# Fills, transposes, first copies, FFN sums and projection steps in another order: a Macaron block on one Trainium2 core

## The chip, the cores and the metric

The kernel runs on one core of one Trainium2 chip. Its time is the device time in microseconds (us) of one execution; several executions give a median. TensorE is called PE, VectorE DVE, ScalarE ACT, GpSimd POOL, SyncE SP, as in the profile; "ACTq" and "SPq" are the queues on which an engine issues DMAs.

## The reference

One Macaron block over x of shape (2, 1024, 256), all in float32:

```python
x = x + 0.5 * ffn(layernorm(x), w_gate, w_up, w_down)
x = x + attention(layernorm(x), Wq, bq, Wk, bk, Wv, bv, Wo, bo)
x = x + 0.5 * ffn(layernorm(x), w_gate, w_up, w_down)

def ffn(x, ...):                       # 256 -> 1024 -> 256
    h = silu(x @ w_gate) * (x @ w_up)
    h = keep_the_2_largest_of_each_4_neighbours_by_magnitude(h)
    return h @ w_down

def attention(x, ...):                 # 32 heads of 8, 8 key/value heads, causal
    q, k, v = x @ Wq + bq, x @ Wk + bk, x @ Wv + bv
    q, k = rope(q), rope(k)
    p = softmax(mask(q @ k.T / sqrt(8)))
    return concat_heads(p @ v) @ Wo + bo
```

## The kernel before

**Data.** The 2048 tokens are four blocks `tb` of 512 tokens; `xs[tb]` holds a block as four tiles of 128 tokens x 256 columns. Blocks 0 and 1 are sequence 0 (b = 0), blocks 2 and 3 sequence 1.

**Stages.** The first FFN (about 0 to 181 us) runs from a written plan: `l` is a layernorm step (`layernorm_T`: statistics on DVE, `rstd` on POOL, normalization into `xn`, eight 128x128 transposes on PE into one PSUM tile `lnT`, a copy to `xnT`); `g` a gate/up step (`gu`, PE; then sg, h, a on ACT and DVE); `m` a mask step on DVE; `d` the down projection (`o`); `a` its sum into x; `p` a step of the attention's beginning. The first `p` fills qT0, kT0 and vaug0 (`rows`, `sequence`, lines 381 to 398) on POOL and then projects q, k and v of sequence 0. Attention follows in 16 units (b, g), one for each key/value head with its four query heads, in rounds of about 25.6 us; then the second FFN, from about 640 us, with the same steps. The down projection of block 3 in the first FFN is left over for round 0 (`down_slowly`, called `beside_first`).

**A round** is written out as a list of operations, `order`: `p1` are scores of the current unit for the row maxima (PE into a "big" PSUM buffer, DVE `maxima`, line 599), `p2` the transposed scores of the unit before it (PE, then an exponential on ACT, line 665, then POOL's causal mask, line 671, where a block is diagonal), `av` the weighted sums of values (PE, line 692), `shift` transposes the maxima (`mT`, line 626), copies them on ACT (`mrow`) and sends them by four DMAs into rows of qT, and `prep` makes the next unit's qT and kT: eight PE transposes (`hT`), a copy on ACT (`stage`, line 524), then 18 DMAs on SP (lines 529 to 545). A round has 18 `p1` operations. In round 0 there is no unit before, so only `p1`, `prep`, one `shift` and the left-over down projection run: after every second `p1`, two steps of `beside_first`, each four matmuls as the program counts pairs, a group of eight matmul records in the trace. Its two sums into x (`add`, line 327) are on DVE.

**Projection of sequence 1.** In rounds 1 to 7 a generator, `project(1, ...)`, is advanced by one step (`a_step`) at certain operations: layernorm statistics (4 steps), rstd (1), normalization on POOL (4), two transposing steps (`lnT`), four additions of bo, and then for each of four tiles a projection step (`pr`, PE; `raw`, DVE; `values`, ACT) and six POOL steps of rope; 43 steps a block, two blocks. Its steps are taken at `shift`, `prep`, `av`, and two of the `p2`: 15 a round. `lnT` and `pr` use the one buffer of pool `ps_tr`, which `shift` uses too:

```python
if n > 0 and (op[0] in ("av", "shift", "prep") or op in (("p2", 2), ("p2", 9))):
    a_step()
```

**What sets the order.** PE and DVE follow the plan in the FFNs; PE and POOL follow the written order in the rounds; elsewhere a scheduler places instructions, and each engine then works strictly in its order. The "big" PSUM pool has three buffers, `ps_tr` and `ps_acc` (sums `o` of the first half, `av`) one each. DMAs on SP and ACT share eight completion counters in turn, so each waits for the one eight places before it.

**The end.** The last operations are `d3 a d3 a a`: the sum of half a block (128 x 512) on DVE, then one DMA of 256 KB to the output.

Of the kernel before, what the change touches and what calls it, by code (L numbers as in the profile page):

```python
# [1 line left out]

# [6 lines left out]
FP = mybir.dt.float32  # L9
# [3 lines left out]
ALU = mybir.AluOpType  # L13
# [3 lines left out]
P = 128  # L17
B, T, C = 2, 1024, 256
NT = B * T
TB = 512  # L20
NTB = NT // TB
NTT = TB // P
# [12 lines left out]
def macaron_kernel(  # L35
# [17 lines left out]
    nc = tc.nc  # L53
# [3 lines left out]
    lnp = ctx.enter_context(tc.tile_pool(name="ln", bufs=2))  # L57
# [5 lines left out]
    xs = [const.tile([P, NTT, C], FP, name=f"x{tb}") for tb in range(NTB)]  # L63
# [98 lines left out]
    def layernorm_T(tb, make, after=None, halves=False, copy=None):  # L162

        xt = xs[tb]
        mv = small.tile([P, NTT, 2], FP, name=f"mv{tb}", tag="mv")
        for t in range(NTT):
            with ExitStack() as order:
                if after:  # L170
                    order.enter_context(tc.issue_after(after()))
                st = small.tile([P, 6], FP, name=f"st{tb}_{t}", tag="st")
                nc.vector.bn_stats(st, xt[:, t, :])
                nc.vector.bn_aggr(mv[:, t, :], st)
            if after:
                yield
        ve = small.tile([P, NTT], FP, name=f"ve{tb}", tag="ve")
        nc.vector.tensor_scalar(ve, mv[:, :, 1], EPS, None, ALU.add)  # L178
        rstd = small.tile([P, NTT], FP, name=f"rstd{tb}", tag="rstd")
        nc.gpsimd.tensor_tensor(rstd, ve, neg_half, ALU.pow)  # L180
        yield
        xn = lnp.tile([P, NTT, C], FP, name=f"xn{tb}", tag="xn")
        for t in range(NTT):
            (nc.gpsimd if after else nc.vector).tensor_scalar(
                xn[:, t, :],
                xt[:, t, :],
                mv[:, t, 0:1],
                rstd[:, t : t + 1],
                ALU.subtract,
                ALU.mult,  # L190
            )
            if after:
                yield
        if not after:
            yield
        dst = make()
        if not after:
            both = ps_big.tile([P, 2, TB], FP, name=f"lnT{tb}", tag="big")
            for kc in range(2):
                for t in range(NTT):  # L200
                    nc.tensor.transpose(  # L201
                        both[:, kc, bass.ts(t, P)], xn[:, t, bass.ts(kc, P)], ident
                    )
            if halves:
                nc.scalar.copy(dst[:, 0, :], both[:, 0, :])  # L205
                nc.vector.tensor_copy(dst[:, 1, :], both[:, 1, :])
            else:
                (copy or nc.scalar.copy)(dst, both)
        else:
            for kc in range(2):  # L210
                tr = ps_tr.tile([P, TB], FP, name=f"lnT{tb}_{kc}", tag="tr")
                for t in range(NTT):
                    nc.tensor.transpose(
                        tr[:, bass.ts(t, P)], xn[:, t, bass.ts(kc, P)], ident
                    )
                nc.scalar.copy(dst[:, kc, :], tr)
                yield
        if not after:
            yield


    class FFN:
# [94 lines left out]
        def down_slowly(self, tb):  # L317

            for t2 in range(2):
                yield from self.down_half(tb, t2, ps_acc, "acc")  # L320
                self.add()

        def add(self):

            tb, t2, o = self.adds.pop(0)
            part = xs[tb][:, bass.ts(t2, 2), :]
            nc.vector.scalar_tensor_tensor(part, o, 0.5, part, ALU.mult, ALU.add)
            if self.store:
                nc.sync.dma_start(
                    out=out[bass.ts(tb, TB), :].rearrange("(t p) c -> p t c", p=P)[  # L330
                        :, bass.ts(t2, 2), :
                    ],
                    in_=part,
                )

        def run(self, plan, gens, outs=()):

# [35 lines left out]
    def attention(actx, beside_first, beside_last, outs):  # L373
# [7 lines left out]
        def rows(pool):  # L381
            i = len(qTs)
            qT = pool.tile([P, REP // 2, T], FP, name=f"qT{i}")
            nc.gpsimd.memset(qT, 0.0)
            qTs.append(qT)
            kT = pool.tile([P, T], FP, name=f"kT{i}")
            nc.gpsimd.memset(kT, 1.0)
            kTs.append(kT)

        def sequence(pool, part_pool):  # L390
            b = len(vaugs)


            vaug = pool.tile([P, NQT, NKV * VW + 32 - VW], FP, name=f"vaug{b}")
            nc.gpsimd.memset(vaug, 1.0)
            vaugs.append(vaug)
            if part_pool:
                parts.append(part_pool.tile([P, NQT, H + NKV, 2 * D], FR, name=f"part{b}"))
# [93 lines left out]
        class Unit:  # L492
# [15 lines left out]
            def prepare(self):  # L508


                s = f"{self.b}_{self.g}"
                tr = ps_big.tile([P, 2, TB], FP, name=f"hT{s}", tag="big")
                src = parts[self.b][:, :, bass.ts(self.g, REP + 1), :]
                for t in range(NQT):

                    nc.tensor.matmul(  # L516
                        out=tr[0 : 2 * GW, t // NTT, bass.ts(t % NTT, P)],
                        lhsT=src[:, t, :, :].rearrange("p h n -> p (h n)"),
                        rhs=ident_r,
                        start=True,  # L520
                        stop=True,
                    )
                hT = early.tile([P, T], FP, name=f"stage{s}", tag="stage")
                nc.scalar.copy(hT[0 : 2 * GW, :], tr[0 : 2 * GW, :, :].rearrange("p i n -> p (i n)"))
                W = 2 * D
                for s in range(2):

                    lo = s * STRIP + ROWS
                    nc.sync.dma_start(
                        out=self.qT[lo : lo + 2, :, :].rearrange("p i (c n) -> p (i c) n", n=TB // 2),  # L530
                        in_=zeros[:, None, :].to_broadcast([2, 2 * REP, TB // 2]),
                    )
                    for j in range(2):
                        for i in range(2):
                            lo = s * STRIP + j * W + i * D
                            nc.sync.dma_start(
                                out=self.kT[lo : lo + D, :],
                                in_=hT[REP * W + j * D : REP * W + j * D + D, :],
                            )
                        lo = s * STRIP + j * W  # L540
                        for pair in range(2):
                            h = 2 * pair + s
                            nc.sync.dma_start(
                                out=self.qT[lo : lo + W, pair, :], in_=hT[h * W : h * W + W, :]
                            )

# [239 lines left out]
        def parsed(order):  # L786
            return [(op[0], *map(int, op[1:])) for op in map(str.split, order.split(";"))]

        ops = parsed(order)
        first = max(i for i, op in enumerate(ops) if op[0] == "p1" and op[1] < 3)  # L790
        units = [(b, g) for b in range(B) for g in range(NKV)]
        made = {}
# [46 lines left out]
        def a_step():  # L839
            while beside and next(beside[0], beside) is beside:  # L840
                beside.pop(0)

        def round_(n, prev, cur):
            nxt = Unit(*units[n + 1]) if n + 1 < len(units) else None
            if n == 1:
                beside.append(second)
            if nxt is not None and nxt.b == 1:
                for _ in second:
                    pass
            firsts = 0  # L850
            for i, op in enumerate(ops):
                step(op, prev, cur, nxt)
                if i == first and cur is not None:
                    cur.negated(0)
                if n == 0 and i == first:

                    nc.scalar.activation(warm, cur.maxima[0][:, 0, 6:7], AF.Exp, scale=0.0)
                if n == 0 and op[0] == "p1":
                    firsts += 1
                    for _ in range(2 * (firsts % 2)):  # L860
                        next(beside_first, None)
                if n > 0 and (op[0] in ("av", "shift", "prep") or op in (("p2", 2), ("p2", 9))):
                    a_step()
                if n > NKV and op == ("av", 5) and divisions:
                    next(divisions.pop(0))
            return cur, nxt
# [138 lines left out]
```

## Time and profile before

| | us |
|---|---|
| median of 3 runs (range) | 828.13 (827.17 to 828.27) |
| the profiled execution | 822.23 |
| its span, first to last instruction | 820.5 |
| mean granted TensorE clock in it | 0.996 |
| PE busy / DVE busy / ACT busy / POOL busy | 781.6 / 655.6 / 426.1 / 235.2 |

The profile is one execution, with every instruction's start and duration. A row of the timeline gives start and duration in us, engine, source line, operation, output and inputs, the number of merged instructions, and in brackets the engine's idle time before it with what ended it. The chain of waits follows the work that ended last back to the start, and adds up its time by engine. "PEclk" or "granted clock" is the share of full TensorE clock that the chip allowed.

### The profile page before, as it was taken

How to read it: one execution, taken by the hardware profiler on the slowest of the kernel's cores; microseconds unless marked ns; L12 is line 12 of the kernel's file. 1: busy time of each engine (PE TensorE's matmuls, PEld its weight loads, DVE VectorE, ACT ScalarE, POOL GpSimd, SP SyncE). 2: the span in 40 equal slices, each digit the busy share in tenths (PEclk: the TensorE clock that was granted, in tenths of full speed). 3: DMA queues.
4: the chain of work that ended last, by engine and by line, in shares of the span. 5: the costliest groups of instructions: out<-in, count | busy, mean ns of one | idle time of the engine just before them, and what ended most of it. 6: DMA issues, size and time to landing. Idle time of an engine off the chain costs nothing.

```text
span 820.5 us, 13946 instructions
## 1 busy us (share of the span) xinstructions
PE 781.6 (95%) x5344; PEld 424.6 (52%) x5344; DVE 655.6 (80%) x870; ACT 426.1 (52%) x529; POOL 235.2 (29%) x443
## 2 busy tenths in 40 slices
PE   4999999999899999999999999999999999999998
PEld 2447574477444544444445444454445445657466
DVE  4797989898968887788889888888885479788692
ACT  1331313211667677768787778878777423122210
POOL 3000193911435555464223322233223100000000
PEclk9999999999999999999999999999999999999999
DMA  8100000022203212311333333322202200000001
GB/s 277 31 0 2 0 2 0 0 39 43 37 21 66 39 45 57 67 25 47 68 68 63 93 73 67 56 46 51 56 30 94 71 1 16 1 26 1 15 11 51
DMA packets 30994, 36.03 MB, mean 44 GB/s; under 512 B 12880, under 2 KB 20944, under 8 KB 30928
## 3 DMA queue, kind: packets, MB, share of 16 engines
q1 hardware_dynamic: 29312, 32.26, 17.6%
q10 hardware_dynamic: 1616, 2.88, 1.0%
q8 instruction: 42, 0.69, 0.3%
q14 instruction: 24, 0.20, 0.1%
HBM read 10.75 MB, written 10.75 MB: 26 GB/s over the span
## 4 chain that ended last, share of the span: by engine, by line
PE 75%; DVE 16%; ACT 4%; POOL 1%; issue 1%; SPq 1%; DMA 1%; DVEq 0%; ACTq 0%; POOLq 0%
PE gu L251 22%; PE av L692 16%; PE o L306 10%; PE s L655 9%; PE s L570 9%; DVE maxima L599 7%; ACT e L665 3%; PE pr L461 2%; PE oo L739 2%; PE lnT L201 1%; PE s L585 1%; PE hT L516 1%; DVE h L291 1%; DVE h L261 1%; DVE sg L260 1%
## 5 line engine op out<-in xcount | busy, mean ns | idle before, releaser
L599 DVE TENSOR_REDUCE maxima<-s 128x2 f32<-128x1024 f32 (+2 forms) x288 | 343.8, 1222 | 62.1 <-PE s L570 44.6
L665 ACT ACTIVATE e<-s 128x1024 f32<-128x1024 f32 x288 | 287.6, 1023 | 93.9 <-PE s L655 86.0
L671 POOL TENSOR_SCALAR_AFFINE_SELECT e<-e 128x256 f32<-128x256 f32 (+1 forms) x224 | 98.2, 451 | 216.7 <-ACT e L665 216.0
L692 PE MATMUL av<-e,vaug 128*32 128x512 f32 (+3 forms) x1536 | 156.6, 496 | 0.0
L570 PE MATMUL s<-kT,qT 64*128 64x512 f32 (+3 forms) x768 | 132.8, 382 | 14.1 <-ACT e L665 11.8
L655 PE MATMUL s<-qT,kT 64*128 64x512 f32 (+3 forms) x768 | 134.2, 394 | 4.4 <-DVE maxima L599 3.5
L251 PE MATMUL gu<-xnT,wg_sb 128*128 128x512 f32 x256 | 121.9, 599 | 0.7 <-ACT xnT L205 0.7
L251 PE MATMUL gu<-xnT,wu_sb 128*128 128x512 f32 x256 | 120.3, 592 | 0.0
L306 PE MATMUL o<-wd_sb,h 128*128 128x256 f32 x512 | 114.4, 381 | 0.1
L570 PEld LDWEIGHTS s<-kT,qT 64*128 64x128 f32 x768 | 68.0, 186 | 81.3 <-ACT e L665 36.8
L306 PEld LDWEIGHTS o<-wd_sb,h 128*128 128x128 f32 x512 | 96.3, 190 | 17.0 <-issue 3.8
L655 PEld LDWEIGHTS s<-qT,kT 64*128 64x128 f32 x768 | 67.2, 185 | 63.5 <-DVE maxima L599 34.3
L259 ACT ACTIVATE sg<-gu 128x512 f32<-128x512 f32 x64 | 38.1, 595 | 117.9 <-PE gu L251 117.9
L262 ACT ACTIVATE a<-h 128x512 f32<-128x512 f32 x64 | 40.3, 630 | 99.4 <-DVE h L261 99.4
L260 DVE TENSOR_TENSOR sg<-sg,gu 128x512 f32<-128x512 f32 x64 | 43.7, 684 | 47.7 <-ACT sg L259 47.6
L251 PEld LDWEIGHTS gu<-xnT,wu_sb 128*128 128x128 f32 x256 | 48.7, 190 | 61.5 <-issue 61.5
L251 PEld LDWEIGHTS gu<-xnT,wg_sb 128*128 128x128 f32 x256 | 48.6, 192 | 54.6 <-issue 49.7
L180 POOL TENSOR_TENSOR rstd<-ve,neg_half 128x4 f32<-128x4 f32 x12 | 12.2, 1016 | 189.7 <-DVE ve L178 187.8
L692 PEld LDWEIGHTS av<-e,vaug 128*32 128x32 f32 x1536 | 34.0, 108 | 49.5 <-issue 37.8
L261 DVE TENSOR_TENSOR h<-sg,gu 128x512 f32<-128x512 f32 x64 | 44.0, 687 | 2.2
L291 DVE SCALAR_TENSOR_TENSOR h<-w,h 128x512 f32<-128x512 bf16 x64 | 44.0, 750 | 0.0
L585 PE MATMUL s<-half_id,half_mask 64*128 64x64 bf16 (+1 forms) x768 | 43.7, 203 | 0.0
(76 smaller groups left out, 562.8 us busy)
## 6 DMA issues: line engine op xcount, KB each, us to landing
qT<-stage SPq DMA_DIRECT2D x128, 64.0 KB
avs<-oT SPq DMA_DIRECT2D x32, 256.0 KB
kT<-stage SPq DMA_DIRECT2D x128, 32.0 KB
qT<-mrow SPq DMA_DIRECT2D x128, 4.0 KB
heads<-avs SPq DMA_DIRECT2D x16, 128.0 KB
out<-x SPq DMA_DIRECT2D x8, 256.0 KB
wu_sb<-in_wu SPq DMA_DIRECT2D x2, 512.0 KB
wg_sb<-in_wg ACTq DMA_DIRECT2D x2, 512.0 KB
```

The source lines that it names most:

```text
L251: nc.tensor.matmul(out=gu[:, i, :], lhsT=w_sb[:, kc, gb, j, :], rhs=self.xnT[tb][:, kc, :], start=(kc == 0), stop=(kc == 1),)
L260: nc.vector.tensor_tensor(sg, sg, gu[:, 0, :], ALU.mult)
L261: nc.vector.tensor_tensor(h[:, j, :], sg, gu[:, 1, :], ALU.mult)
L291: nc.vector.scalar_tensor_tensor(h[:, j, :], w[:, j, :], at, h[:, j, :], op, ALU.mult)
L306: nc.tensor.matmul(out=o[:, i, :], lhsT=self.hms[tb][k // 4][:, k % 4, bass.ts(2 * t2 + i, P)], rhs=self.wd_sb[:, k // 4, k % 4, :], start ...
L570: nc.tensor.matmul(out=to[:, i, s, bass.ds(col, n)], lhsT=self.qT[strip, pair, bass.ts(qt, P)].bitcast(FR), rhs=self.kT[strip, bass.ds(kc ...
L585: nc.tensor.matmul(out=last.rearrange("p (t n) -> p t n", n=P)[:, :, bass.ts(h, STRIP)], lhsT=half_mask[strip, h, :], rhs=half_id[strip, N ...
L599: ins = nc.vector.tensor_reduce(dst, src, AX.X, ALU.max, negate=True)
L655: nc.tensor.matmul(out=to[:, i, s, bass.ds(col, n)], lhsT=self.kT[strip, bass.ts(kb, P)].bitcast(FR), rhs=self.qT[strip, pair, bass.ds(q0, ...
L665: nc.scalar.activation(e, to, AF.Exp, scale=SCALE)
L671: nc.gpsimd.affine_select(out=first, in_=first, pattern=[[0, 2], [0, len(pairs)], [1, P]], compare_op=ALU.is_ge, fill=0.0, base=0, channel ...
L692: nc.tensor.matmul(out=self.av[32 * i : 32 * i + 32, TB - n : TB], lhsT=vaugs[self.b][:, kb, bass.ds(self.g * VW, 32)], rhs=es[i][:, bass. ...
```

## The change

1. In `layernorm_T` the eight transposes of a block go tile by tile (t outside, kc inside) instead of one 128-column half after the other.
2. kT0 and vaug0 are filled by DVE instead of POOL.
3. The DMAs that build the first unit's qT and kT go to SP and ACT in turn; those of all other units stay on SP.
4. The two sums of the down projection in round 0 are a scaled copy on ACT and an addition on POOL instead of one DVE instruction. Of its steps, those after the 13th `p1` and later run after the round's last operation.
5. In rounds 1 to 7 no projection step follows `shift` or the two `p2` any more; two follow each of `av` 1, 3, 5 and 7. There are still 15 a round.
6. The last sum of the kernel, and its store, are made for each 128-token tile by itself.

In the built program the fills of kT0 and vaug0 stand on DVE between the fill of `zeros` (right after the sum of `o_0_1`) and the statistics of the attention's first layernorm. On ACT one of the `zeros` DMAs stands in the middle of the first FFN; of the others one stands between the copy `stage_0` and the last Abs, and seven behind that. On PE the last two groups of `o_3_1` stand between the last `p1` of round 0 and the first `p2` of round 1.

```diff
@@ layernorm_T
-            for kc in range(2):
-                for t in range(NTT):
+            for t in range(NTT):
+                for kc in range(2):
                     nc.tensor.transpose(
                         both[:, kc, bass.ts(t, P)], xn[:, t, bass.ts(kc, P)], ident
                     )
@@ FFN.down_slowly
-                self.add()
+                self.add_aside()
+
+        def add_aside(self):
+            tb, t2, o = self.adds.pop(0)
+            part = xs[tb][:, bass.ts(t2, 2), :]
+            half = lnp.tile([P, NTT, C], FP, name=f"half{tb}_{t2}", tag="xn")[:, 0:2, :]
+            nc.scalar.mul(half, o, 0.5)
+            nc.gpsimd.tensor_tensor(part, part, half, ALU.add)
@@ FFN.add
-            part = xs[tb][:, bass.ts(t2, 2), :]
-            nc.vector.scalar_tensor_tensor(part, o, 0.5, part, ALU.mult, ALU.add)
-            if self.store:
-                nc.sync.dma_start(out=..., in_=part)
+            last = self.store and tb == NTB - 1 and t2 == 1
+            for i in range(0, 2, 1 if last else 2):
+                n = 1 if last else 2
+                tiles = bass.ds(2 * t2 + i, n)
+                part = xs[tb][:, tiles, :]
+                nc.vector.scalar_tensor_tensor(
+                    part, o[:, i : i + n, :], 0.5, part, ALU.mult, ALU.add
+                )
+                if self.store:
+                    nc.sync.dma_start(out=..., in_=part)
@@ rows, sequence
-            nc.gpsimd.memset(kT, 1.0)
+            (nc.vector if i == 0 else nc.gpsimd).memset(kT, 1.0)
-            nc.gpsimd.memset(vaug, 1.0)
+            (nc.vector if b == 0 else nc.gpsimd).memset(vaug, 1.0)
@@ Unit.prepare
+                queues = itertools.cycle([nc.sync] if self.b or self.g else [nc.sync, nc.scalar])
-                    nc.sync.dma_start(     # zeros, kT and qT alike
+                    next(queues).dma_start(
@@ round_
+        PAIRS = [("av", k) for k in (1, 3, 5, 7)]
                 if n == 0 and op[0] == "p1":
                     firsts += 1
-                    for _ in range(2 * (firsts % 2)):
-                        next(beside_first, None)
-                if n > 0 and (op[0] in ("av", "shift", "prep") or op in (("p2", 2), ("p2", 9))):
-                    a_step()
+                    if firsts <= 12:
+                        for _ in range(2 * (firsts % 2)):
+                            next(beside_first, None)
+                if n > 0:
+                    for _ in range(2 if op in PAIRS else op[0] in ("av", "prep")):
+                        a_step()
```

## The prediction

> **What bounds the kernel now.** I read the page first, its busy times and its chain of waits.
>
> ```profile
> PE 781.6 (95%) x5344; PEld 424.6 (52%) x5344; DVE 655.6 (80%) x870; ACT 426.1 (52%) x529; POOL 235.2 (29%) x443
> ...
> PE 75%; DVE 16%; ACT 4%; POOL 1%; issue 1%; SPq 1%; DMA 1%; DVEq 0%; ACTq 0%; POOLq 0%
> ```
>
> TensorE (PE) is the bound, so an edit pays only where PE waits or runs at a lower clock. The table of windows, by stage, shows where that is (columns: us, then busy time of PE, PEld, DVE, ACT, POOL with counts, granted clock, DMA share, GB/s):
>
> ```profile
> 0.00:12.70 12.70, 2.29 (x8) 1.48 (x8) 5.09 (x16) 2.07 (x3) 6.92 (x19) 1.00 0.85 310
> 12.70:181.20 168.50, 168.44 (x529) 96.40 (x529) 146.05 (x242) 45.83 (x78) 54.64 (x61) 1.00 0.09 19
> 181.20:207.50 26.30, 24.40 (x173) 17.78 (x172) 22.20 (x24) 3.07 (x4) 6.46 (x7) 1.00 0.24 39
> ```
>
> PE is idle until its first transpose and then full for 168 us: what the head saves, the first FFN passes on whole. The head in the timeline, and the rows of tile xn there (min/median/max in ns):
>
> ```profile
> 7.93 0.95 POOL L387 MEMSET kT<- 128x1024 f32 x1
> 8.01 2.65 DVE L184 TENSOR_SCALAR xn<-x,mv,rstd 128x256 f32<-128x256 f32 x4 [1.09 <-POOL rstd L180]
> 8.82 0.73 POOL L395 MEMSET vaug<- 128x760 f32 x1
> ...
> 9.75 2.29 PE L201 MATMUL lnT<-ident,xn 128*128 128x128 f32 x8 [9.75 <-DVE xn L184]
> ```
>
> ```profile
> L184 DVE TENSOR_SCALAR xn<-x,mv,rstd x4: 394/400/1681, 8.0 to 10.3; 128x256 f32<-128x256 f32 x4
> ```
>
> One of four equal normalizations takes 1681 ns instead of 400: the first, which ends at 9.69, just after POOL's two fills (9.55).
>
> Next, PE's waits in the timeline, in round 0 and at its end:
>
> ```profile
> 182.54 0.88 PE L570 MATMUL s<-kT,qT 64*128 64x256 f32 x3 [0.98 <-DMA kT<-stage]
> ...
> 207.54 0.50 PE L655 MATMUL s<-qT,kT 64*128 64x512 f32 x2 [0.95 <-DVE maxima L599]
> 208.67 0.81 PE L570 MATMUL s<-kT,qT 64*128 64x256 f32 x4 [0.63 <-DVE maxima L599]
> ...
> 209.80 0.56 PE L655 MATMUL s<-qT,kT 64*128 64x512 f32 x2 [0.19 <-DVE maxima L599]
> ```
>
> and in round 2, with a projection step that runs 2.78 us where its like take 1.56:
>
> ```profile
> 239.57 0.41 PE L626 MATMUL mT<-ident_r,ms 128*8 128x128 f32 x4 [0.35 <-POOL ms L403]
> 240.64 2.78 PE L461 MATMUL pr<-wqkv_sb,xnTa 128*128 128x384 f32 x4 [0.66 <-ACT mrow L634]
> ```
>
> The windows around both places show why:
>
> ```profile
> 206.70:210.10 3.40, 1.74 (x16) 1.30 (x18) 3.40 (x6) 1.02 (x1) 0.01 (x1) 1.00 0.00 0
> 210.10:213.50 3.40, 3.40 (x26) 2.28 (x23) 3.29 (x5) 2.52 (x3) 1.54 (x5) 0.50 0.02 6
> 216.90:220.30 3.40, 2.28 (x24) 0.90 (x16) 3.40 (x8) 2.31 (x3) 1.67 (x2) 1.00 0.51 77
> 237.40:240.80 3.40, 1.92 (x23) 1.11 (x20) 2.65 (x4) 2.51 (x3) 2.79 (x7) 1.00 0.06 15
> 240.80:244.20 3.40, 3.40 (x10) 1.72 (x12) 0.56 (x1) 0.15 (x1) 0.00 (x0) 0.50 0.02 5
> ```
>
> After 3.4 us with PE idle for 1.66 or 1.48, the granted clock is 0.50 for 3.4 us; 1.12 idle left it at 1.00. Such a dip costs up to 1.7 us where PE is the bound.
>
> **The sum, part by part**, against the profiled execution (span 820.5, time 822.23). The median of the runs, 828.13, lies 5.9 higher for a reason that the profile doesn't show; I carry the difference over unchanged.
>
> *Head.* Without the fills the first xn should take 0.40: 1681 - 400 = 1.28 us off the path. Transposes tile by tile: now four of them follow DVE at its pitch of 0.32 and four more run behind at 0.21; in the new order two fit behind each xn, and only one is left behind the last: 0.7 off. Together -2.0 (-1.2 to -2.3, the first half alone or a little more). The weights landed at 7.6 and earlier, so nothing else becomes late. The fills of kT and vaug now stand on DVE behind the sum of o_0_1, at 79 us; DVE fills 2x256 in 0.27, so 1024 and 760 columns take 1.07 + 0.80 = 1.9 us. Behind them the next statistics (and POOL's rstd), then sg and h; DVE has gaps of 0.82 at 81 and 2.76 at 102, and PE, with three big PSUM buffers, waits for none of it between: taken as 0; without this cover it would be 1.0. In later layernorms xn is long done when PE transposes: 0.
>
> *First unit's copies on two queues.* SP issues 16 of them in 10.4 us (0.65 for kT, 0.56 for qT), 170.8 to 181.2. With half on ACT's queue (one ahead of the last Abs, L262, seven behind it; a wait of 8 DMAs' distance stands before each) both queues are through some 5 us earlier, and PE's 0.98 wait goes. What is late next is the sum of o_2_0, which frees the accumulator at 182.6 where PE's first group of sums starts at 183.49: -0.8 (0 to -1.0). ACT's seven issues delay nothing: it is idle from 173.5 to 188.8.
> [...]
>
> *FFN sums of round 0.* Eight groups of 1.92 us follow every second p1 step; now six do, and the last two come after the eighteenth. At the round's end this fills PE's 0.95 + 0.63 + 0.19 (-1.8) and takes away the first dip (-1.7). But DVE now sets the pace from the twelfth step: its tenth maximum starts near 198, and the eighteenth step needs the PSUM buffer that the fifteenth maximum frees, 6 x 1.13 + 0.4 later, at 205.2; PE, with steps of 0.3 to 0.5 after the sixth group's end at 200.06, would be there at 202.25. New waits: 2.95, plus 0.25 behind the sums: +3.2. More than 1.5 us idle in so short a stretch is what the two dips followed, so I count a new dip at 201 to 206, partly under DVE's pace: +1.2 (0 to +1.7). Net +0.9 (-0.3 to +2.6). The two sums themselves move from DVE (0.69 each) to an ACT copy (0.59 for that size) and a POOL add (0.75 for 128x256, so about 1.5); ACT is idle there, and the half of o_3_0 frees the accumulator within PE's next two steps: 0.
>
> *Projection steps, rounds 1 to 7.* Still 15 a round, none behind a shift now, two behind av 1, 3, 5 and 7. A projection's PSUM buffer is the one that the shift's rows are copied from; its waits for that copy, 0.66 at 240.64 and 0.76 at 339.11, go: -1.4 (-0.7 to -1.4). With the first the window before 240.8 has 0.8 idle, and the second dip goes: -1.6 (0 to -1.7). The layernorm statistics stand between more maxima; DVE's late ones cost PE 0.57 + 0.58 in round 1 and 0.21 + 0.37 + 0.25, and POOL's ms 0.40, in round 4: I take -0.9 of these 2.4 (0 to -2.0). New: in round 1 both lnT halves fall on av 5, and the second waits until ACT, behind an exponential of 1.02, has copied the first (0.59): +0.9 (0 to +1.2). In rounds 3 and 5 pairs hold a projection and its turn, so POOL stands until DVE has made raw, with the next masks behind it; those are needed 4 us later. Unseen waits of such pairs: +0.3 (-0.5 to +2; PE's waits of rounds 1 to 7 above a later round's are 7 us in all).
>
> *The end.* The last add waits for the whole PSUM tile either way.
>
> ```profile
> 816.71 0.69 DVE L327 SCALAR_TENSOR_TENSOR x<-o,x 128x512 f32<-128x512 f32 x1 [6.21 <-PE o L306]
> 817.43 0.37 SPq L329 DMA_DIRECT2D out<-x  x1
> ```
>
> Two adds of 0.4 let the second store be issued at about 817.55, 0.1 later, but with half the bytes: the whole store's packets lie between 818.3 and 819.2, so 0.45 less: -0.3 (-0.5 to +0.3).
>
> Sum: -2.0 - 0.8 + 0.9 - 1.4 - 1.6 - 0.9 + 0.9 + 0.3 - 0.3 = -4.9: a profile near 817.3 and a median of **823.2 us**. Its own range is 820 to 826.5.
>
> **Rivals.**
> *The clock is not set by idle time.* Then the two dips stay, and -1.7, +1.2 and -1.6 are struck: -2.8, 825.3. For: two dips are few to learn from. Against: both follow the two idlest stretches after 182 us, and 1.12 idle gave none.
> [...]
>
> *Slower: a dip in every projection round.* Steps that stood alone gave PE work between its waits; as pairs they leave stretches without any (no step from the second p2 steps to av 0 but two). If a window of each of rounds 1 to 6 passes about 1.3 idle, that is 6 x 1.7 = 10.2 on top: +5.3, 833.4. It decides from four dips on (4.9 + 1.7, over 1.7 each). For: 1.48 idle was enough. Against: the later rounds, with no such steps, keep the clock at 1.00.
>
> *The fills are not what slows the first xn* (the change does less than it says: the loads that saturate the DMA there do it). Then 1.3 is missing: -3.6, 824.5. Against: the other three xn, under the same loads, take 0.40.
>
> **How the numbers follow.** Forecast 0.50, dips stay 0.20, dips in each round 0.15, fills innocent 0.05; 0.10 that several costs reach their upper ends and cancel the gain, near 828. A measurement of this kernel can tell about 0.2% (1.7 us) from no change. Faster by more: 0.47 + 0.15 + 0.05 + 0.03 = 0.70. Slower: 0.15 + 0.04 = 0.19. Within: 0.11. All terms at their best give 818.5, all at their worst 832; I cut the upper side at 830.5, which leaves out the dips in each round and a little more.
>
> **What would show it.** Right: all four xn at 0.40 and the first gu near 10.7; no DMA wait before round 0; PE waits of about 3 us on maxima before the last two groups of sums, clock 0.5 near there; full clock around the first projection of round 2; no wait of pr on mrow; a wait of the second lnT in round 1. Wrong: a first xn of still 1.7, PE in FFN 0 waiting on DVE, or windows at 0.5 in rounds 1 to 6.

## The result, and the profile after

| | before | after |
|---|---|---|
| median on the same chip, 22 runs each | 825.64 us | 821.78 us |
| range | 822.40 to 828.27 | 820.15 to 824.90 |
| the profiled execution: time, span, mean granted clock | 822.23, 820.5, 0.996 | 824.67, 822.9, 0.990 |

The ratio is 0.9962, with a 95% interval of 0.9948 to 0.9976: faster by 0.38%, which is the ratio of the means (825.28 and 822.14); the medians lie 3.9 us apart (0.47%), as both kernels' runs fall into groups. The two profiled executions say the opposite, 2.4 us longer after. Both are right; much of this section and of the experiments is about how that can be.

The page of after, its busy times and its chain of waits:

```profile
PE 786.1 (96%) x5344; PEld 426.4 (52%) x5344; DVE 654.7 (80%) x871; ACT 426.9 (52%) x531; POOL 236.2 (29%) x443
...
PE 71%; DVE 22%; ACT 4%; issue 1%; POOL 1%; DMA 0%; DVEq 0%; ACTq 0%
```

The count of PE's instructions is the same, its busy time 4.5 us more: the same matmuls at a lower mean clock, 0.990 against 0.996. DVE's share of the chain has gone from 16% to 22%, SPq and the DMAs have left it. The head, in the timeline of after:

```profile
7.99 1.38 DVE L185 TENSOR_SCALAR xn<-x,mv,rstd 128x256 f32<-128x256 f32 x4 [1.09 <-POOL rstd L181]
8.46 1.97 PE L202 MATMUL lnT<-ident,xn 128*128 128x128 f32 x8 [8.46 <-DVE xn L185]
11.11 3.78 PE L252 MATMUL gu<-xnT,wg_sb 128*128 128x512 f32 x4 [0.68 <-ACT xnT L206]
```

All four xn now take 0.40 and less, and the first gu starts 1.61 earlier (12.72 before). Round 0, same view, PE's rows and one of DVE:

```profile
181.85 1.99 PE L307 MATMUL o<-wd_sb,h 128*128 128x256 f32 x8 [0.84 <-DVE x L340]
...
200.40 0.50 PE L584 MATMUL s<-kT,qT 64*128 64x512 f32 x2 [0.78 <-DVE maxima L613]
201.53 0.49 PE L584 MATMUL s<-kT,qT 64*128 64x512 f32 x2 [0.63 <-DVE maxima L613]
202.66 0.80 PE L584 MATMUL s<-kT,qT 64*128 64x384 f32 x4 [0.63 <-DVE maxima L613]
...
204.51 6.14 PE L307 MATMUL o<-wd_sb,h 128*128 128x256 f32 x16
```

```profile
211.49 3.73 DVE L613 TENSOR_REDUCE maxima<-s 128x4 f32<-128x1024 f32 x3 [4.15 <-PE s L599]
```

The wait for the copies (0.98) is gone, and the wait for the sum of o_2_0 (0.84) stands in its place. Three waits for DVE's maxima precede the last `p1`; the two groups of sums behind it take 6.14 instead of 3.84; and DVE then stands idle for 4.15 until the next round's first scores come. The table of windows shows the clock (columns as before):

```profile
199.20:202.60 3.40, 1.42 (x8) 0.37 (x4) 3.40 (x4) 0.00 (x0) 0.00 (x0) 1.00 0.14 24
202.60:206.00 3.40, 3.25 (x14) 2.19 (x15) 3.40 (x5) 0.00 (x0) 0.00 (x0) 0.50 0.02 5
206.00:209.40 3.40, 3.40 (x10) 2.68 (x9) 1.34 (x3) 0.00 (x0) 0.00 (x0) 0.50 0.00 0
305.00:308.40 3.40, 2.72 (x24) 1.34 (x22) 3.40 (x5) 2.21 (x3) 2.30 (x5) 1.00 0.51 78
308.40:311.80 3.40, 3.40 (x24) 1.43 (x26) 2.73 (x3) 2.47 (x3) 3.40 (x4) 0.50 0.52 82
```

Half clock for two stretches after the waits of round 0; once more at 308, after only 0.68 of idle time; and for two stretches from 465.4, in round 10, which the change does not touch. Before had two stretches in all, up to PE's last matmul.

### The profile page after: what moved, and what is told of

Same layout as the page of the kernel before. It is cut to its first block, busy times and chain, and to the rows that moved or that the text cites. A ratio compares the mean times of both kernels' runs of the same rounds, so it can differ in the third digit from the quotient of the medians.

```text
span 822.9 us, 13949 instructions
## 1 busy us (share of the span) xinstructions
PE 786.1 (96%) x5344; PEld 426.4 (52%) x5344; DVE 654.7 (80%) x871; ACT 426.9 (52%) x531; POOL 236.2 (29%) x443
## 4 chain that ended last, share of the span: by engine, by line
PE 71%; DVE 22%; ACT 4%; issue 1%; POOL 1%; DMA 0%; DVEq 0%; ACTq 0%
PE gu L252 20%; PE av L706 16%; PE s L584 9%; PE s L669 9%; PE o L307 9%; DVE maxima L613 8%; ACT e L679 3%; DVE h L292 2%; PE pr L474 2%; PE oo L753 2%; DVE h L262 1%; DVE sg L261 1%; DVE b L275 1%; PE s L599 1%; PE hT L529 1%
## 5 line engine op out<-in xcount | busy, mean ns | idle before, releaser
L706 PE MATMUL av<-e,vaug 128*32 128x512 f32 (+3 forms) x1536 | 158.5, 501 | 0.0
L307 PE MATMUL o<-wd_sb,h 128*128 128x256 f32 x512 | 116.6, 386 | 0.9 <-DVE x L340 0.8
L307 PEld LDWEIGHTS o<-wd_sb,h 128*128 128x128 f32 x512 | 98.1, 193 | 18.5 <-issue 3.7
```

Source lines behind the costliest of these rows:

```text
L307: nc.tensor.matmul(out=o[:, i, :], lhsT=self.hms[tb][k // 4][:, k % 4, bass.ts(2 * t2 + i, P)], rhs=self.wd_sb[:, k // 4, k % 4, :], start ...
L706: nc.tensor.matmul(out=self.av[32 * i : 32 * i + 32, TB - n : TB], lhsT=vaugs[self.b][:, kb, bass.ds(self.g * VW, 32)], rhs=es[i][:, bass. ...
```

## The experiments

"First s to shift 1 of round 2" is the time from round 0's first scores to the first transposition of row maxima in round 2 (that of half 1, `shift 1`; round 0 has `shift 0` alone), with the number of half-clock stretches of 3.4 us in it in brackets. It holds what parts 3 and 4 of the change do directly. Medians are of 6 to 29 runs (e10 to e12 were run once each and are not in the table); beside e1 to e4 the kernel before had 825.72, beside e5 to e8 825.43, beside e9 823.53.

| kernel | median us | ratio to before (95%) | profile: first s | first s to shift 1 of round 2 |
|---|---|---|---|---|
| before | 823.5 to 825.7 | 1 | 181.18 | 58.39 (1) |
| after | 821.78 | 0.9962 (0.9948 to 0.9976) | 180.37 | 60.88 (2) |
| e1 head only | 823.06 | 0.9992 (0.9971 to 1.0014) | 181.45 | 58.80 (2) |
| e2 sums only | 827.19 | 1.0024 (1.0004 to 1.0044) | 181.61 | 61.35 (2) |
| e3 after, sums at old places | 818.81 | 0.9931 (0.9906 to 0.9957) | 180.08 | 58.45 (2) |
| e4 after, steps at old places | 825.37 | 1.0008 (0.9987 to 1.0029) | 180.11 | 60.83 (2) |
| e5 after, PE's waits filled | 820.31 | 0.9949 (0.9931 to 0.9967) | 180.28 | 59.61 (0) |
| e6 sums in halves | 819.76 | 0.9937 (0.9918 to 0.9955) | 180.92 | 60.00 (0) |
| e7 e3 with other pairs | 821.97 | 0.9958 (0.9936 to 0.9979) | 180.13 | 59.27 (2) |
| e8 after, one queue | 821.62 | 0.9967 (0.9952 to 0.9983) | 180.38 | 61.18 (2) |
| e9 sums after even steps | 817.69 | 0.9921 (0.9893 to 0.9949) | 179.72 | 56.56 (0) |

### e1: the head alone

The kernel before with parts 1 and 2 of the change (transposes by tile, fills on DVE).

> The kernel before with the new order of transposes and the two fills on DVE, nothing else. My theory: the head is on the path, and PE starts its first gate/up matmul 1.6 us earlier, as in the trace of after; up to half of that is lost again where the clock warms up later, so 0.8 to 1.6 us faster than before. Rival (what the head saves is waited for later, behind DVE's two fills): within 0.3 us of before. The runs spread with the number of half-clock stretches in each, so fastest runs are compared too.

The medians (825.72 and 823.06) lie 2.7 apart, but the interval reaches from 2.4 us faster to 1.2 slower: inconclusive. Fastest against fastest it is 822.21 against 822.61, and among the runs with a mean clock of 0.994 the medians are 822.8 and 823.2: some 0.4, less than expected. The profile says why it is hard to see. From the first xn to the first gu it takes 3.11 (4.71 before), as hoped; yet round 0 starts at 181.45, no earlier than before. The granted clock rose to 1.00 at 16.74 here, 5.4 us after the first gu, and at 15.55 before, 2.8 us after it. The additional 2.6 us at half clock cost, by an estimate, half of that, 1.3. (The trace has no record of the clock before its first rise, and the views print 1.00 there; the gu matmuls show the half clock, for in the first profiles of before and after they start every 0.85 us before the rise and every 0.43 after it.)

### e10: the fills alone

```diff
-            nc.gpsimd.memset(kT, 1.0)
+            (nc.vector if i == 0 else nc.gpsimd).memset(kT, 1.0)
```

and the same for vaug, on the kernel before.

> The kernel before with the first fills of kT and vaug on DVE and nothing else. The prediction's theory (the fills slow the first xn): the four xn take 1.38 together as in the changed kernel (2.65 before), PE's lnT starts 1.28 earlier against the first xn's start, and the transposes keep their 2.29. Rival (the load traffic slows it): 2.65 stays. The stretch from the first xn to the first gu, 4.71 before and 3.12 changed, is 3.4 by the theory.

The timeline of this run:

```profile
8.05 1.39 DVE L184 TENSOR_SCALAR xn<-x,mv,rstd 128x256 f32<-128x256 f32 x4 [1.09 <-POOL rstd L180]
8.52 2.30 PE L201 MATMUL lnT<-ident,xn 128*128 128x128 f32 x8 [8.52 <-DVE xn L184]
```

The fills were what slowed the first xn: 2.65 falls to 1.39 and the first gu, at 11.50, comes 3.45 after the first xn. The rival (the load traffic) falls. The other order of the transposes is then worth 3.45 - 3.12 = 0.33: lnT 1.97 instead of 2.30. One run gave 828.0 at a mean clock of 0.988, which says nothing about the fills.

### e2 and e3: the sums, alone and undone

e2 is the kernel before with part 4 alone; e3 is the changed kernel with the steps where they were, still with ACT's copy and POOL's addition:

```diff
-                    if firsts <= 12:
-                        for _ in range(2 * (firsts % 2)):
-                            next(beside_first, None)
+                    for _ in range(2 * (firsts % 2)):
+                        next(beside_first, None)
```

> The kernel before with the last two groups of FFN sums after round 0 and the two additions on ACT and POOL, nothing else. My theory: PE starves in the last third of round 0 (waits of about 2 us on maxima), the clock halves and the sums run in it: 0 to 2.5 us slower than before. Rival (the sums fill PE's waits at the round's end and the clock stays up there): 2 to 3.5 us faster.

> The kernel after, with the last two groups of sums back at their old places inside round 0 (the additions stay on ACT and POOL). My theory: no starving in round 0; the profile has PE waits under 1 us between steps 12 and 18, and the time is 1 to 3 us below that of after. Rival (late sums are what the change gains by): 1 to 3 us above after, close to before less the head.

Alone, the new places made the kernel 1.5 us slower in the median (0.24%, interval above 1); undone in the changed kernel they gave 3.0 back. The intervals of after and e3, 0.9948 to 0.9976 and 0.9906 to 0.9957, overlap by little, and four of e3's six runs lie under the fastest of after (820.15). The timeline of e3 at the same place, PE and DVE:

```profile
205.38 0.50 PE L669 MATMUL s<-qT,kT 64*128 64x512 f32 x2 [0.67 <-DVE maxima L613]
206.51 0.84 PE L584 MATMUL s<-kT,qT 64*128 64x256 f32 x4 [0.63 <-DVE maxima L613]
207.64 0.50 PE L669 MATMUL s<-qT,kT 64*128 64x512 f32 x2 [0.16 <-DVE maxima L613]
```

```profile
210.60 1.23 DVE L613 TENSOR_REDUCE maxima<-s 128x8 f32<-128x1024 f32 x1 [0.54 <-PE s L599]
```

PE waits 1.46 for maxima here and 2.04 in the changed kernel, not far apart. The difference is on DVE: its longest idle time behind the last sums is 0.54 in e3, 4.15 after. DVE paces this stretch, and while PE works off two groups of sums behind the last step, DVE has nothing. In the kernel before, DVE has no idle time at all beside PE's three waits at the end of round 0 (207.54 to 209.80); its timeline there:

```profile
205.67 0.68 DVE L327 SCALAR_TENSOR_TENSOR x<-o,x 128x512 f32<-128x512 f32 x1
206.27 3.48 DVE L599 TENSOR_REDUCE maxima<-s 128x2 f32<-128x1024 f32 x3
...
209.88 2.35 DVE L599 TENSOR_REDUCE maxima<-s 128x4 f32<-128x1024 f32 x2
```

### e5: PE's waits filled

The changed kernel, and after each of steps 14 to 17 two extra matmuls whose results nobody uses (the definition of `fill_in` is left out):

```diff
+                    elif 14 <= firsts < 18:
+                        fill_in()     # 2 x matmul 128x256 into the unused half of o
```

> The changed kernel with two extra matmuls of 128x256 (results unused) after each of the steps p1 14 to 17 of round 0, in PE's waits of 0.78, 0.63 and 0.63 on DVE's maxima. Nothing else is moved, and DVE's pace stays. Theory (the granted clock falls when PE is idle for too much of a stretch of 3.4 us, also when the idle time is in pieces): no row of 0.50 between 199 and 210, the last two groups of sums at 1.92 instead of 3.07 each, shift 1 of round 1 some 2 us earlier than 212.7, and the time 1 to 2.5 us under the changed kernel's 821.8. Rival (the clock falls for another reason, such as the end of a long stretch at full load): the 0.50 stays, the filler matmuls only take the place of the waits, and the time is 821.8 to 822.5.

The windows that were at half clock after, and the row of the two groups of sums in the timeline:

```profile
199.00:202.40 3.40, 3.40 (x16) 1.84 (x14) 3.36 (x3) 0.00 (x0) 0.00 (x0) 1.00 0.14 25
202.40:205.80 3.40, 3.40 (x21) 2.18 (x20) 3.40 (x4) 0.00 (x0) 0.00 (x0) 1.00 0.02 5
205.80:209.20 3.40, 3.40 (x16) 2.73 (x15) 1.47 (x4) 0.00 (x0) 0.00 (x0) 1.00 0.02 5
```

```profile
205.57 3.72 PE L321 MATMUL o<-wd_sb,h 128*128 128x256 f32 x16
```

With nothing done but work that is thrown away, PE has no idle time in these windows, the clock stays at 1.00 and the groups take 3.72 instead of 6.14. So at this place the half clock went with PE's idle time, though that lay in pieces of 0.78, 0.63 and 0.63. The place of the clock's grid (e11 and e12 below) does not explain it: the grid stands at 1.05 here and at 1.06 in e8, whose clock falls at 202.44 (its scores of 0.51 at 201.14 take 0.67 at 202.28 and 0.80 at 204.54). Shift 1 of round 1 comes at 211.36, 1.35 earlier and not 2, and the median is 1.5 lower. DVE still stood idle 2.87 us behind the groups, and at full clock throughout e5 takes 59.61 where e9, with the groups inside, takes 56.56: the clock is the smaller part of what their place costs.

### e9 and e6: the groups later, and in halves

e9 has all eight groups inside, after the even steps; e6 has sixteen halves, one after each of steps 3 to 18, and the pairs of e7. The lines added, in place of the three that e3 takes out:

```diff
+                    for _ in range(2 * (1 - firsts % 2) * (firsts <= 16)):    # e9
+                        next(beside_first, None)
+                    if firsts > 2:                                             # e6
+                        next(beside_first, None)
```

> The changed kernel with all eight groups of sums among the p1 steps, as in the kernel before, but after the even ones (2 to 16) instead of the odd ones (1 to 15). Theory (PE's idle time in one stretch of 3.4 us decides the clock, and a group placed later fills a wait on DVE): the wait of 0.84 on the sum of o_2_0 falls to 0.3 to 0.5, the waits of 0.67, 0.63 and 0.16 on maxima at the end of round 0 to about 0.9 together, and the clock stays at 1.00 there; first s to shift 1 of round 2, 58.45 with the odd places, 56.5 to 57.5; 816.5 to 818 in the median, under the 818.8 of the odd places. Rival (the next round's first step waits for the later group, as it did behind step 18): 58.5 to 59.5, 819 to 820.

> The changed kernel, but the sums of round 0 in halves of 0.96 us, one after each of the steps p1 3 to 18 (instead of pairs of halves after every second step up to 11 and two groups behind the last), and the pairs of projection steps at av 1, 3, 4 and 7. Theory (DVE paces round 0, so work for PE must be spread as evenly as DVE's maxima come): the wait of 0.84 on the sum of o_2_0 goes, the three waits on maxima (2.04) and the dip behind them (about 1.9) go, and so does the second lnT's 0.68; 816 to 818. Rival (DVE's 18 maxima of 1.13 are the bound of round 0 in any order, the waits turn up behind shift 0 or at the first exponentials): about as with the sums at their old places, 818.5 to 820.

PE's rows of e9 in the timeline:

```profile
181.19 1.99 PE L307 MATMUL o<-wd_sb,h 128*128 128x256 f32 x8 [0.53 <-DVE x L340]
...
205.58 0.84 PE L584 MATMUL s<-kT,qT 64*128 64x256 f32 x4 [0.80 <-DVE maxima L613]
206.71 0.50 PE L669 MATMUL s<-qT,kT 64*128 64x512 f32 x2 [0.16 <-DVE maxima L613]
```

Nearly as the theory had it: 0.53 for o_2_0, 0.96 for maxima, full clock, 56.56, and a median of 817.69. This is the best version that was run; its slowest run, 819.71, lies under the fastest of after, 820.15, but its interval overlaps that of e3: that it beats both kernels is shown, that it beats e3 is not.

In e6 the waits named went, and so did the dip, but the first maxima now cost 0.60 and 0.34 (PE's waits up to shift 1 are 2.3 together, as in e3), and round 1 had e7's new wait instead of the 0.68. Still, the waits do not explain 60.00; the median, 819.76, is what the rival expected. The groups of PE in round 0 (182 to 208) tell where it went; e3 first, then e6 (64 matmuls each, three records of e6 are missing):

```profile
L307 PE MATMUL o<-wd_sb,h 128*128 128x256 f32 x64 | 16.0, 392 | 0.9 <-DVE x L340 0.9
```

```profile
L307 PE MATMUL o<-wd_sb,h 128*128 128x256 f32 x61 | 17.4, 406 | 0.4 <-ACT half L329 0.3 <-DVE x L340 0.2
```

A half followed by a step takes 1.06 until the step's scores start (187.40 to 188.46), half of a whole group 0.97, and a step alone 0.51 instead of 0.45: some 0.15 for each of the sixteen halves with its step, 2.4 us, which is about the difference to e3's shift 1 of round 1 (30.70 against 28.43 after the first s). PE's busy time up to there says the same: 28.41 in e6, 25.96 in e3, both at full clock. Neither theory had PE's own time growing; why it grows is open.

### e4: the projection steps undone

```diff
-                    for _ in range(2 if op in PAIRS else op[0] in ("av", "prep")):
+                    if op[0] in ("av", "shift", "prep") or op in (("p2", 2), ("p2", 9)):
                         a_step()
```

> The kernel after, with the projection steps of rounds 1 to 7 at their old operations (shift, prep, each av, two of the p2). My theory: the new places take away two waits of a projection for the copied rows (1.4 us) and waits for maxima, so this one is 1.5 to 3.5 us slower than after, with the waits of pr for mrow back in its profile. Rival (the gain is in the head and the queues): within 0.5 us of after.

The median is 3.6 above the changed kernel's, just past the range expected. The predicted wait is back (timeline of e4, round 2):

```profile
240.94 0.41 PE L640 MATMUL mT<-ident_r,ms 128*8 128x128 f32 x4 [0.36 <-POOL ms L416]
242.01 1.56 PE L474 MATMUL pr<-wqkv_sb,xnTa 128*128 128x384 f32 x4 [0.66 <-ACT mrow L648]
```

After has neither of them; a wait of 0.21 on maxima stands in its round 2 instead. Between shifts 1, and without half clock, rounds 2, 4 and 5 take 31.09, 29.68 and 29.45 with the old places (round 5 from before, as e4 has a dip there) and 30.57, 29.01 and 28.77 with the new (second profile of after): 1.9 in three rounds. Runs with the same mean clock, 0.994, differ by as much: 823.69 to 825.43 in e4, 821.77 to 823.42 in after. The rest of the 3.6 goes with more dips: e4's profile has one at 338.8, behind 0.97 of idle time (window 335.40 to 338.80), where after has none.

### e7: other pairs

e3 with pairs at `av` 1, 3, 4 and 7.

> The changed kernel with the sums of round 0 at their old places and the pairs of projection steps at av 1, 3, 4 and 7 instead of 1, 3, 5 and 7, so that the two lnT halves of round 1 stand in different places. Theory (each wait of PE counts by itself): the second lnT's wait of 0.68 in round 1 goes and nothing comes; 0.4 to 0.8 under the 818.8 of the run with the sums at their old places: 818.0 to 818.4. Rival (steps closer together wait for each other: a projection behind its statistics): 818.8 to 820.

Neither came: 821.97, 3.2 above e3. In round 1 the second lnT's wait of 0.68 went, and in its place stands a wait for the normalization on POOL:

```profile
229.09 0.33 PE L214 MATMUL lnT<-ident,xn 128*128 128x128 f32 x1 [0.87 <-POOL xn L185]
```

Round 1 is 0.84 longer than in e3, rounds 2 to 7 are equal. That leaves 2.3 us of the difference. With a mean clock of 0.996 the two kernels take the same time (818.33 and 818.62 here, 818.32 to 818.88 in e3); but six of e7's eight runs had a mean clock of 0.990 to 0.992, two of e3's six, and its one profile (818.62, 0.996) is not of these. Why its clock falls more often is open.

### e8: one queue again

```diff
-                queues = itertools.cycle([nc.sync] if self.b or self.g else [nc.sync, nc.scalar])
+                queues = itertools.cycle([nc.sync])
```

> The changed kernel with all sixteen copies of the first unit on SP's queue again. Theory of the prediction (the copies' end sets when round 0 starts): a wait for the copies of 0.9 to 1.0 is back at the second s group, in place of the 0.84 for the sum of o_2_0; the first group of sums 0.8 us later than 181.85; 822.2 to 822.8. Rival (DVE paces round 0 from its twelfth step, so 0.8 at its start only shortens the waits on maxima): the waits of 2.04 on maxima shrink by as much, and the time stays within 0.3 of 821.8.

```profile
181.72 0.82 PE L584 MATMUL s<-kT,qT 64*128 64x256 f32 x3 [0.97 <-DMA kT<-stage]
...
201.14 0.51 PE L584 MATMUL s<-kT,qT 64*128 64x512 f32 x2 [0.78 <-DVE maxima L613]
202.28 0.67 PE L584 MATMUL s<-kT,qT 64*128 64x512 f32 x2 [0.63 <-DVE maxima L613]
203.41 0.80 PE L584 MATMUL s<-kT,qT 64*128 64x384 f32 x4 [0.46 <-DVE maxima L613]
```

The wait for the copies is back and the first group 0.75 later, as the prediction had it; the waits on maxima shrink by 0.17 only; 61.18 against 60.88, so 0.3 of the 0.75 is left. Yet the median is 821.62 against 821.78: on the clock of the whole kernel the second queue gave nothing that these runs can tell. The rival's number is right and its reason only in small part.

### e11 and e12: both kernels once more

Nothing altered, for a second profile of each.

> The changed kernel once more, with nothing altered, for a second profile. Theory (the clock is decided in stretches of 3.413 us on a grid of its own, whose place against the kernel's start differs from run to run): PE's waits stand where they stood (0.84, 0.78, 0.63, 0.63, 0.68), every change of the granted clock lies on one grid of 3.413 us, that grid lies elsewhere against the first instruction than in the first profile (1.22), and other waits are followed by 0.50: not all of those near 202, 308 and 465. Rival (the dips belong to the kernel's own places): 0.50 from 202.6, 308.4 and 465.4 again.

> The kernel before once more, with nothing altered. By the grid theory its clock changes lie on one grid again, elsewhere than 1.90, and the number of half-clock stretches of 3.413 us tells the time: some 822.5 with two to four of them, 826 to 828.5 with five or more. Rival: two dips at 210 and 241 again, whatever the time.

The windows of after, second profile:

```profile
201.60:205.00 3.40, 1.63 (x13) 0.79 (x14) 3.40 (x4) 0.00 (x0) 0.00 (x0) 1.00 0.04 8
205.00:208.40 3.40, 3.40 (x8) 2.46 (x9) 3.40 (x5) 0.00 (x0) 0.00 (x0) 0.50 0.00 0
304.00:307.40 3.40, 2.83 (x26) 1.06 (x24) 3.40 (x5) 2.21 (x3) 1.90 (x3) 1.00 0.48 71
307.40:310.80 3.40, 3.28 (x40) 1.72 (x38) 3.37 (x4) 3.25 (x4) 2.91 (x5) 1.00 0.53 83
```

and of before, second profile:

```profile
182.80:186.20 3.40, 2.37 (x18) 1.80 (x18) 3.02 (x5) 0.00 (x0) 3.17 (x3) 1.00 0.24 39
186.20:189.60 3.40, 3.40 (x16) 2.19 (x15) 1.14 (x2) 0.00 (x0) 2.84 (x3) 0.50 0.08 16
240.80:244.20 3.40, 2.92 (x37) 1.53 (x34) 2.61 (x5) 2.63 (x3) 3.02 (x6) 1.00 0.08 17
244.20:247.60 3.40, 2.40 (x14) 1.41 (x16) 1.96 (x3) 0.91 (x2) 0.99 (x3) 1.00 0.01 2
```

After, again: the same waits on maxima (0.78, 0.63, 0.64 and a fourth of 0.49) and on o_2_0 (0.84), but one stretch at half clock up to PE's last matmul instead of five, none at 308 or 465, and 820.55 us instead of 824.67. Before, again: 825.66 instead of 822.23, with a dip at 186 after the wait for the copies, 1.02 (0.98 in the first profile, with no dip behind it), three stretches from 213.5, and none at 241. The changes of the granted clock lie on one grid in each of these profiles: in the first profile of before they are 194.56, 3.413, 27.307 and 3.413 us apart, in that of after 187.733, 6.827, 98.987, 3.413, 153.6 and 6.827, all whole multiples of 3.413. Counted from the kernel's start the grid stands at 1.22 and 0.23 in the two profiles of after and at 1.90 and 1.85 in those of before. So the theory holds for after, and the rival falls in both. For before two expectations missed: the grid stood almost where it had been, and four stretches at half clock up to PE's last matmul should have made some 822.5, not 825.66. With this small shift the clock's first rise moved. Of the stretch 12.1 to 15.5, the first layernorm's end leaves PE idle for 0.58 in one profile and 0.66 in the other; the clock rose at 15.55 in the one and a whole stretch later, at 18.92, in the other. (After's first rise, at 14.87, followed a stretch without idle time; in its second profile the stretch from 10.47 to 13.88, with 0.63 idle, was not followed by the rise, which came at 17.29.) Round 0 then starts 1.67 later (182.85 against 181.18), which a count of the later stretches leaves out, and other waits share a stretch of the grid.

## Why the prediction was right, point by point

The direction and the order of size were right: 4.9 us faster was forecast, 3.9 came. That the predicted 823.2 lies 1.4 from the measured 821.78 is in part luck, since two errors met.

- **The base.** The 5.9 us between the median of before and its profile were carried over as unexplained. They go with half-clock stretches and with a later first rise of the clock (in e12 the later rise alone makes some 1.67 us): before's runs fall in two groups, 822.6 to 823.6 with a mean clock of 0.994 to 0.996, and 826.4 to 828.5 with 0.988 to 0.990 (14 and 14 of the 29 beside e1 to e4). All three runs shown were of the second. The comparison's own base is 825.64, so the forecast's time started 2.5 too high.
- **Head, -2.0.** Right in kind, 1.61 at the first gu: the fills gave 1.26 (1.28 put), the transposes 0.33 (0.7 put; lnT ends 1.06 behind the last xn, so about four transposes stand there and not one). But "what the head saves, the first FFN passes on whole" did not hold, as PE works at half clock until the clock's first rise (15.55 before, 14.87 after; gu every 0.85 us until then, every 0.43 behind it). What reaches round 0 is less and varies: its first scores start 0.81 earlier in the first profiles of both kernels and 1.26 in the second, as the rise did not come a fixed time after the first gu: 2.83 behind it before and 3.76 after, 6.17 and 6.19 in the second profiles. The fills' cover on DVE held nearly: they took 0.91 and 0.69, and PE waits 0.29, 0.30 and 0.41 for an xn at 133 to 134 in both profiles of after and in e10; in e9, with the same fills, and in before it does not.
- **Copies on two queues, -0.8.** In place as said: 0.98 gone, the sum of o_2_0 next, with 0.84. In time 0.3 by the profiles up to round 2, and nothing in the medians (e8). Issue time was not small here: SP's sixteen issues in e8 last from 169.93 to 180.36, and the wait of 0.97 is real; another took its place.
- **Sums of round 0, +0.9.** The failed step. The waits on maxima were forecast at 2.95 and came at 2.04, the dip came, two stretches long; but undoing the move gave 3.0 (e3). Wrong was the credit, "at the round's end this fills PE's 0.95 + 0.63 + 0.19 (-1.8) and takes away the first dip (-1.7)". Those waits were DVE's pace: DVE was busy without a gap beside them (rows under e3), so PE's time there was not on the path. The two groups behind the last step are on it, for DVE gets no scores meanwhile (4.15 idle). Nor did the clock gain: e3 has two stretches at half clock behind round 0, and after has two. The term was +1.5 (e2, beside the kernel before) to +3.0 (e3).
- **Projection steps, -2.7.** Right, and under-sized: 3.6 by e4. The waits of pr are gone; rounds 2, 4 and 5 are 1.9 shorter; the dip of round 2 is gone and others are rarer. The new wait of the second lnT was 0.68 (0.9 put). It cost nothing on the whole: round 1 takes 28.5 in e4 and after, since its waits on maxima fell from 2.24 to 1.01.
- **The end, -0.3.** From PE's last instruction to the end of the span 3.84 before, 3.75 after: -0.1.
- **The rivals.** That the clock is not set by idle time fell with e5. The prediction counted on dips from some 1.3 to 1.5 us of idle time; of eleven dips (two in before, three in after, two in e12, one each in e3, e4, e9 and e11) six followed 0.68 to 1.23, the others 1.48 to 1.99. Dips in each round did not come all the same: rounds 1 to 6 of after show one in the first profile and none in the second. The fills' innocence fell with e10.
- **Not tested.** The end's two stores, and the sums on ACT and POOL by themselves, were in no run alone.

## What to carry to other kernels

A wait of the engine with the most work is worth removing only if that engine is late there: at the end of round 0 DVE set the pace, so taking PE's work out of an earlier place to fill its waits there gained nothing, and that work, put behind the last step, starved DVE. Spread such work so that the pacing engine never runs dry (e9), but not finer than needed, for in e6 each half of a group with its step cost PE 0.15 us more. And before reading two profiles against each other, compare when the clock first rises and count the half-clock stretches in both, for here the slower kernel had the shorter profile.

## What the runs showed that was not expected

- The clock fell without any long gap: at 308.42 in after it fell behind 0.68 us of idle PE time in pieces of at most 0.33, while the longest single gap of before, 0.98 at 181.57, was followed by none. In the first profiles of both kernels, from the clock's rise to 800 us, the stretches of the grid with 1.48, 1.66 and 1.99 us of idle time were followed by half clock; of nineteen with 0.67 to 1.23, two were (0.68 and 1.23, both in after); of those with up to 0.63, none was the start of a dip. What decides between is open, and so is the length of a dip: one stretch in before, one or two in after, three in e12 from 213.5, with PE busy for 3.25 to 3.40 of each 3.40 (2.99 in e4's).
- With nothing altered the same kernel took 820.15 to 824.90, and the mean clock sorts the runs: 0.998 took 820.15 to 820.63 (6 runs), 0.994 and 0.995 820.43 to 823.42 (10), 0.990 824.07 to 824.90 (6). From the fastest group to the slowest that is some 1.0 us for each of four more stretches, but the first rise of the clock, 17.29 in the profile with one stretch and 14.87 in that with five, is mixed into it. In the traces a stretch cost 0.7 to 1.4 us by its place: 1.4 at 308 in after (round 4 took 30.44 there and 29.01 in the second profile), and 0.7 for each of the two behind round 0 in e3 (30.02 from shift 1 of round 1 to that of round 2, 28.53 in e5, which has none).
- Fewer dips are a gain of their own: e3's run with a mean clock of 1.000 took 816.93, its three with 0.996 took 818.32 to 818.88, and its two with 0.992 took 820.56 and 820.67.
